# Two transformer layers on one core: the blocks' queries, keys and values in buffers of their own, and an earlier schedule for the attention sums

## The chip, the cores and the metric

One AWS Trainium2 chip, of which the kernel uses one core. A core has a matrix engine (TensorE; PE in the profile, its weight loads PEld), a vector engine (VectorE, DVE), a scalar engine (ScalarE, ACT), a general engine (GpSimd, POOL) and SyncE (SP), which here only issues transfers. Each engine works through its own list of instructions in order; semaphores tie the lists together. The metric is the device time of one launch in microseconds (us), as a median over runs. Tensors in use lie in on-chip memory of 128 partitions (SBUF), products of TensorE in a small accumulator memory (PSUM).

## The reference

The input `x` has 4 sequences of 1024 positions with 256 channels. Two layers follow each other, each added to its input:

```python
x = x + attention(layernorm(x))      # 16 heads of 16, causal, ALiBi bias, softmax over the positions
x = x + ffn(layernorm(x))

def ffn(x):                           # x: (4, 1024, 256); its attention runs along the FIRST axis
    q, k, v = split(x @ in_proj_w.T + in_proj_b)
    scores = einsum('tbhd,sbhd->bhts', q, k) / 4   # each of 1024 positions: 4 tokens among themselves
    ctx = softmax(scores) @ v
    h = layernorm(x + ctx @ out_w.T + out_b)
    probs = softmax(h @ router_w.T + router_b)     # 8 experts
    assign = max(index of the two largest)         # one expert for each token
    oe = gelu(h @ w1[assign].T + b1) @ w2[assign].T + b2
    return layernorm(h + oe)
```

The second layer therefore has two parts: an attention in which at each of the 1024 positions only its four tokens (one of each sequence) see each other, which is element-wise work of the vector engine, and a mixture of experts in which each of the 4096 tokens goes to exactly one of eight small networks (256 to 256 to 256).

## The kernel before

All of it is in `fast_layer`. (A general version, for inputs whose softmax sums leave a safe range, stands behind it in a branch that is not taken.)

**First layer.** Attention is cut into units: a chunk of 256 query positions of one sequence (16 of them); those of the last chunk are cut once more into blocks of 128, so there are 20 units. Each unit has four groups of four heads and, by the length of its keys, one or more rounds; there are 160 rounds in all. A round is `score` (TensorE makes scores `sk` from `slots`, ScalarE exponentiates them to `p`, GpSimd masks the diagonal at line 1005) and, two rounds at a time, `weigh` (TensorE multiplies `p` by the values `v`, ScalarE copies the result to `yt`). The values carry a column of ones, so the softmax's sums come out as rows of the same product. When a unit's last product is out, its result is normalised through DRAM in steps:

- `load_sums` (line 1064) stores `y` and loads the sums back in another layout, on SP's queue;
- `invert` (line 1071) takes reciprocals on VectorE and stores them (`r`, SP);
- `load_y` (line 1079) loads the reciprocals, spread over channels (`su`), and the unit's result (`yc`): four transfers on SP;
- `divide` (line 1096) multiplies `yc` by `su` on VectorE;
- `project` (line 1105) multiplies by the output weights on TensorE (`op`) and adds to `x` on VectorE.

SP's queue also carries the loads of keys and queries into `slots` (line 958) and the stores of keys. The very last unit is normalised on chip instead (`normalise`: a product `sum` with a constant, a reciprocal and a multiply for each group, `yn`; then `project_slots`).

**Second layer.** Positions are cut into 8 blocks of 128 positions with 4 tokens each. `front(i)` (line 1573) is a Python generator for one block; it yields between its stages and says which engine the next one needs: `E` and `P` for VectorE, `N` and `A` for ScalarE, `R` for GpSimd, `D` (and `d` for further pieces of the same) for TensorE. Its stages are in order: layer norm of `x` to `u`; transposes (`ut`); projection in four pieces, one for each token (`qkvp`, copied to `qkv`), where the first piece is of kind `DQ`; four score stages, one for each token t (a multiply `pr` and a reduce to `sc`); softmax over the four; four weighted products (`pv`, multiply and adds, to `ctx`); transposes (`ct`), output projection (`ao`), layer norm and the choice of the expert (`key`, `rank`, `hot`). In the last block (i = 7) some work stands differently: the values are projected between the score stages and ScalarE makes all copies, and TensorE sums the halves of the weighted products (`ctp`). A `DQ` piece may only be placed when no earlier block holds the flag `held["qkv"]`, since there is one `qkv` buffer of 4 x 776 floats in each partition. The block sets the flag at its `DQ` and takes it off after its fourth weighted product.

**Third part.** After 6 blocks have been placed, `tabulate_first` builds a table of 18 tiles of 128 tokens with equal expert; after the last block `tabulate_rest` builds the table of the other 20 (`counts_all`, `who`, `at_t`). Each of the 38 tiles is gathered (`given`, line 1839, an indirect transfer on GpSimd), transposed (`mtp`), multiplied (`hid`), put through gelu (`ge`), multiplied (`oe`), normalised (`o`) and scattered (`out_dram`, line 1955).

**What sets the order.** The order of instructions on every engine is fixed when the kernel is built, by a planner written in the kernel (main loop from line 2270). It goes through the 160 rounds in pairs and keeps estimated times of PE, DVE and ACT. Around the rounds it has places for vector work (`E_slot`, line 2219) and for TensorE work (`D_slot`, line 2231). At each place it issues what is due: the steps above of each unit, at set allowances after the unit's last product (the constants of line 76, in the planner's microseconds: sums 7, inverse 14, loads 18, multiply 29, projection 31), and then stages of at most two running blocks, vector ones by `take_E` (line 2076) and TensorE ones by `take_D` (line 2100). A block enters the queue when all four units over its positions are projected. So the allowances also set when blocks can begin.

After the last round the steps still due are issued, then groups 2 and 3 of the last unit are normalised (lines 2294 to 2301), and a second planner interleaves what is left: block 7, whatever of block 6 and of the first table is unfinished, and the tiles of the experts. There, the loads of the experts' weights stand on SP, for all experts in two layers (`w1`, `w2`) and for the first four tiles as sets of their own.

Of the kernel before, what the change touches and what calls it, by code (L numbers as in the profile page):

```python
# [37 lines left out]
P = 128  # L38
# [6 lines left out]
QC = 512  # L45
# [27 lines left out]
D_SLOT = 10.0  # L73
SWITCH, COLUMN, EXP_AT_ALL, EXP, READ = 0.2, 1 / 600, 0.17, 1 / 1200, 0.7
AHEAD, EARLY_BY, ROOT, OF_D = 1.0, 0.2, 1.4, 0.35
SUMS_BY, INVERTED_BY, Y_BY, DIVIDED_BY, PROJECTED_BY = 7.0, 14.0, 18.0, 29.0, 31.0

EXP_ZERO = -126 * math.log(2.0)

# [526 lines left out]
def fast_layer(ctx: ExitStack, tc: tile.TileContext, odd, x, wq, wk, wv, wp, w_in, w_out, w_r,  # L606
# [119 lines left out]
    def wide(a):  # L726
        return a.unsqueeze(1).to_broadcast([P, B] + list(a.shape)[1:])
# [4 lines left out]
    at_row = con(Q_ROW)  # L732
    number_i = const("number_i", [P, 1], I32)
    nc.gpsimd.iota(number_i, pattern=[[0, 1]], base=0, channel_multiplier=1)
    pos = fact.tile([P, T], F32, tag="pr", name="pos", bufs=2)
    nc.gpsimd.iota(
        pos, pattern=[[1, T]], base=-T // 2, channel_multiplier=0,
        allow_small_or_imprecise_dtypes=True,
# [728 lines left out]
    def prepare_biases(stage):  # L1467

        if stage == 0:
            b1_rows = fact.tile([E, C], F32, tag="equal", name="b1_rows")
            nc.scalar.dma_start(
                b1_rows.rearrange("e (c p) -> e c p", p=P),
                b1.rearrange("p (e c) -> e c p", c=CC),
            )
            b2_rows = fact.tile([E, C], F32, tag="before", name="b2_rows")
            nc.scalar.dma_start(b2_rows, b2)
            b_row = fact.tile([1, 2 * C], F32, tag="u", name="b_row", bufs=2)
            for k, at in enumerate((B_IN, B_OUT)):  # L1480
                nc.scalar.dma_start(
                    b_row[:, k * C:(k + 1) * C], rows[at:at + C].unsqueeze(0)
                )
            held["biases"] = (
                (b1_rows, b_bf[0]), (b2_rows, b_bf[1]),
                (b_row[:, :C], in_bf), (b_row[:, C:], out_bf),
            )
            return
        src, three = held["biases"][stage - 1]
        if three is out_bf:  # L1490
            nc.vector.tensor_tensor(src, src, router["passed"][0:1, :C], ALU.add)
        n, width = src.shape
        rest = fact.tile([n, width], F32, tag="pr", name="rest", bufs=2)
        nc.vector.tensor_copy(rest, src)
        pieces = fact.tile([n, 3, width], BF16, tag="turned", name="pieces", bufs=TURNED)
        for k in range(3):
            nc.vector.tensor_copy(pieces[:, k], rest)
            nc.sync.dma_start(three[k * n:(k + 1) * n, :width], pieces[:, k])
            if k < 2:
                nc.vector.tensor_tensor(rest, rest, pieces[:, k], ALU.subtract)  # L1500
# [72 lines left out]
    def front(i, fact, more, last):  # L1573
# [43 lines left out]
            for_later(t)  # L1617
        store(("x", i), store_later)
        yield "DQ" if more else "D", 2.8
        qkv = fact.tile([P, B, 3 * C + E], F32, tag="qkv", name=f"qkv_{i}")  # L1620

        def projected_qkv(t, lo, hi):
            pq = bank(f"qkvp_{i}_{t}")[:, :hi - lo]
            for cc in range(CC):
                nc.tensor.matmul(
                    pq, ut[:, cc, t * P:(t + 1) * P], w_in_sb[:, cc, lo:hi],
                    start=cc == 0, stop=cc == CC - 1,
                )
                if not lo + cc:
                    nc.tensor.matmul(pq[:, :C], ones_bf, in_bf, start=False, stop=False)  # L1630
            if lo and not last:
                nc.vector.tensor_copy(qkv[:, t, lo:hi], pq)
            else:
                nc.scalar.copy(qkv[:, t, lo:hi], pq)

        for t in range(B):
            projected_qkv(t, 0, QC)
# [4 lines left out]

        def routed():
            nc.vector.tensor_tensor(
                u_[:, :, C:], qkv[:, :, 3 * C:], wide(router["b_out"]), ALU.add
            )

        if not last:
# [4 lines left out]
        for t in range(B):  # L1653
            yield "E", 2.4, 0.9 if last else 0.0
            if last:
                projected_qkv(t, QC, 3 * C + E)
            pr = fact.tile([P, B, C], F32, tag="pr", name=f"pr_{i}_{t}", bufs=2)
            nc.vector.tensor_tensor(pr, wide(qkv[:, t, 0:C]), qkv[:, :, C:2 * C], ALU.mult)
            nc.vector.tensor_reduce(
                sc[:, t], pr.rearrange("p s (h d) -> p s h d", d=D), AX.X, ALU.add  # L1660
            )
        yield "E", 1.1
        over_s = lambda a: a.rearrange("p t s h -> p t h s")
        top = small.tile([P, B, H], F32, tag="top", name=f"top_{i}", bufs=1)
# [11 lines left out]
        nc.vector.tensor_tensor(sc, sc, each_s(tot), ALU.mult)  # L1676

        def weighted(t):
            pr = fact.tile([P, B, C], F32, tag="pr", name=f"pv_{i}_{t}", bufs=2)
            nc.vector.tensor_tensor(  # L1680
                pr.rearrange("p s (h d) -> p s h d", d=D),
                qkv[:, :, 2 * C:3 * C].rearrange("p s (h d) -> p s h d", d=D),
                sc[:, t].unsqueeze(3).to_broadcast([P, B, H, D]),
                ALU.mult,
            )
            return pr
# [26 lines left out]
        else:  # L1713
            ctx_ = fact.tile([P, B, C], F32, tag="ctx", name=f"ctx_{i}")
            for t in range(B):
# [1 line left out]
                pr = weighted(t)  # L1717
                nc.vector.tensor_tensor(pr[:, 0:2], pr[:, 0:2], pr[:, 2:4], ALU.add)
                nc.vector.tensor_tensor(ctx_[:, t], pr[:, 0], pr[:, 1], ALU.add)
        if more:  # L1720
            held.pop(("qkv",))
        if not last:
            if i < PC * (NC - 2):
                yield "N", 0
# [337 lines left out]
    def product(cost, what):  # L2062
        taken.clear()
        what()
        end = on_tensor(cost)
        busy("DVE", OF_D * cost, end - 0.5 * cost)
        read_at(max(end + READ, time["DVE"]))
        return end
# [28 lines left out]
                if it.kind == "end":  # L2097
                    running.remove(it)

    def take_D(cost):  # L2100

        for it in list(running):
            while it.kind[0] in "Dd":
                if it.kind == "DQ" and ("qkv",) in held:
                    break
                if it.kind != "d" and it.ready > time["PE"] + EARLY_BY:
                    break
                if cost and cost + it.cost > D_SLOT:
                    break
                if it.kind == "DQ":  # L2110
                    held["qkv",] = True
                cost += it.cost
                end = product(it.cost, it.next)
                it.ready = max(end + READ, time["DVE"])
            if it.kind == "end":
                running.remove(it)

    begins = [0]
# [109 lines left out]
            experts.fetch()  # L2228
        take_E(some)

    def D_slot(p):
        todo = of_D.pop(p, []) + pop_due(due_D, time["PE"])
        for cost, what in todo:
            product(cost, what)
        take_D(sum(cost for cost, _ in todo))

    for p in range(-6, 0):
        E_slot(2 * p)
# [34 lines left out]
    for p in range(len(rounds) // 2):  # L2273
        then = p < len(rounds) // 2 - 1
        score_next(2 * p)
        E_slot(2 * p)
        D_slot(p)
        fill()
        take_E(then)
        score_next(2 * p + 1)  # L2280
        if len(waiting) > 2:
            weigh_next(waiting[:2])
            del waiting[:2]
        fill()
        E_slot(2 * p + 1, then)
# [5 lines left out]


    assert not of_E and not of_D, (sorted(of_E), sorted(of_D))
    for _, what in pop_due(due_E + [], 1e9) + pop_due(due_D + [], 1e9):
        what()
    for it in running:
        it.ready = 0.0
    for g in range(2, G):
        normalise(g)
    load_sums(last_unit)  # L2300
    project_slots()
    tail = ctx.enter_context(pool("tail", 1))
# [205 lines left out]
```

## Time and profile before

| | |
|---|---|
| median of 3 runs (lowest to highest) | 827.63 us (824.45 to 828.9) |
| the profiled execution | 827.67 us |
| its span in the profile | 825.9 us |
| mean granted TensorE clock | 0.949 of full speed |
| busy: PE / weight loads / DVE / ACT / POOL | 708.6 / 532.4 / 544.8 / 416.5 / 253.6 us |
| last product of the attention's rounds ends | 620.4 us |
| block 7's first score multiply begins | 666.91 us |
| first gather of the second table | 734.32 us |

The span is the time from the first to the last instruction of the profiled execution; the device time of the same execution is 1.8 us longer. Busy times are averages over stages that differ a lot, so each stage has to be looked at by itself: 0 to 620 us is the first layer's attention with the blocks 0 to 6 of the second layer set in between; 620 to 734 is the rest of blocks 6 and 7 with the tiles of the first table; from 734 on there are only tiles. `L587` is the line of a helper through which nearly all instructions of the compute engines pass, so they are told apart by the names of their tiles. Names are written as out<-in.

### The profile page before, as it was taken

The page shows a single profiled execution, that of the slowest core. Times are in us where ns is not written, and L with a number is a line of the kernel's source. Part 1 is how long each engine was busy: PE and PEld are TensorE (multiplying, and loading weights), DVE is VectorE, ACT ScalarE, POOL GpSimd, SP SyncE. Part 2 cuts the span into 40 slices and gives each one's busy share as a digit, 9 for nine tenths or more (in the row PEclk, how much of TensorE's full clock was granted, in tenths as well). Part 3 has the DMA queues.
Part 4 walks back from the last instruction along what each step waited for, and adds up shares of the span by engine and source line. Part 5 has one row for each costly group of instructions (what it writes and reads, how often), then busy time and mean ns, then how long its engine had stood idle before and what let it go on. Part 6 is the DMA issues. An engine that isn't in the chain of part 4 may idle for free. (4 is left out here: it accounts for less than half of the span.)

```text
span 825.9 us, 22497 instructions
## 1 busy us (share of the span) xinstructions
PE 708.6 (86%) x8917; PEld 532.4 (64%) x8917; DVE 544.8 (66%) x1316; ACT 416.5 (50%) x625; POOL 253.6 (31%) x360
## 2 busy tenths in 40 slices
PE   3988878999999999998998998999983689677882
PEld 2766656667666656565787876788662368566771
DVE  7335403739489768847966648497684779885663
ACT  1554535647547656635665757487550236233540
POOL 5533211313021222111222211122120235638885
PEclk9899898999999999999999999999995699988996
DMA  7444444435234234423554556255125512234430
GB/s 218 120 149 147 115 126 139 137 98 169 82 105 136 91 97 127 131 74 98 140 157 118 163 162 158 57 156 166 36 75 198 178 47 89 89 96 127 128 97 25
DMA packets 75220, 99.57 MB, mean 121 GB/s; under 512 B 19496, under 2 KB 58723, under 8 KB 74596
## 3 DMA queue, kind: packets, MB, share of 16 engines
q1 hardware_dynamic: 62272, 67.84, 28.3%
q10 hardware_dynamic: 7972, 16.05, 6.2%
q0 software_dynamic: 4864, 14.16, 5.7%
q8 instruction: 73, 1.20, 0.7%
q14 instruction: 39, 0.32, 0.1%
HBM read 61.55 MB, written 35.12 MB: 117 GB/s over the span
## 5 line engine op out<-in xcount | busy, mean ns | idle before, releaser
L587 ACT ACTIVATE p<-sk 128x1024 f32<-128x1024 f32 (+1 forms) x320 | 287.8, 939 | 160.6 <-PE sk L587 139.4
L1005 POOL TENSOR_SCALAR_AFFINE_SELECT p<-p 128x512 f32<-128x512 f32 (+1 forms) x160 | 105.6, 664 | 396.6 <-ACT p L587 394.6
L587 PE MATMUL sk<-slots 32*128 32x128 f32 (+1 forms) x3456 | 181.1, 328 | 21.5 <-DVE kq L587 8.4
L587 PEld LDWEIGHTS sk<-slots 32*128 32x128 f32 x3456 | 137.2, 187 | 65.0 <-issue 24.8
L587 PE MATMUL pv<-p,v 128*32 128x128 f32 (+1 forms) x3456 | 143.4, 312 | 9.9 <-DVE count L587 2.9
L587 PEld LDWEIGHTS pv<-p,v 128*32 128x32 f32 x3456 | 95.9, 110 | 46.9 <-issue 7.8
L587 PE MATMUL qkvp<-w_in,ut 128*128 128x264 f32 (+1 forms) x228 | 80.3, 488 | 0.0
L587 PEld LDWEIGHTS qkvp<-w_in,ut 128*128 128x128 f32 x228 | 40.8, 193 | 26.9 <-issue 22.4
L587 PE MATMUL oe<-w,ge 128*128 (+1 forms) x152 | 43.4, 410 | 14.4 <-DVE given L587 6.0
L587 PE MATMUL qkp<-xt,wqk 128*128 128x256 f32 x224 | 55.5, 392 | 0.2 <-ACT p L587 0.2
L1839 POOL DMA_INDIRECT given<-rows,rows x38 | 43.5, 1144 | 27.4 <-DVE at_t L587 11.4
L587 DVE COPY qkv<-qkvp 128x264 f32<-128x264 f32 x28 | 12.1, 432 | 54.1 <-PE qkvp L587 54.1
L587 PEld LDWEIGHTS qkp<-xt,wqk 128*128 128x128 f32 x224 | 40.9, 191 | 10.5 <-issue 3.3
L587 PE MATMUL hid<-mt,w 128*128 128x128 f32 x304 | 47.2, 293 | 0.4 <-ACT ge L587 0.4
L587 ACT COPY qkv<-qkvp 128x512 f32<-128x512 f32 (+1 forms) x29 | 16.1, 557 | 59.0 <-PE qkvp L587 47.1
L587 PEld LDWEIGHTS hid<-mt,w 128*128 128x128 f32 x304 | 42.2, 201 | 1.9 <-ACT ge L587 0.9
L1955 POOL DMA_INDIRECT out_dram<-o,out_rows x38 | 38.9, 1024 | 8.7 <-issue 5.9
L587 DVE TENSOR_TENSOR pv<-qkv,sc 128x1024 f32<-128x1024 f32 x32 | 40.2, 1257 | 0.6 <-PE ctp L587 0.6
L587 DVE TENSOR_REDUCE sc<-pr 128x64 f32<-128x1024 f32 x32 | 39.0, 1220 | 1.1
L587 DVE TENSOR_TENSOR pr<-qkv 128x1024 f32<-128x1024 f32 x32 | 39.6, 1238 | 0.0
L587 PEld LDWEIGHTS oe<-w,ge 128*128 128x128 f32 x152 | 27.2, 200 | 19.1 <-DVE given L587 7.4
L587 PE MATMUL vp<-wv,xt 128*128 128x256 f32 x128 | 34.4, 414 | 0.0
(316 smaller groups left out, 1017.9 us busy)
## 6 DMA issues: line engine op xcount, KB each, us to landing
slots<-k SPq DMA_DIRECT2D x128, 80.0 KB
k<-kq SPq DMA_DIRECT2D x32, 256.0 KB
v<-v ACTq DMA_DIRECT2D x4, 1152.0 KB
x<-in_x_dram SPq DMA_DIRECT2D x16, 256.0 KB
y<-yt SPq DMA_DIRECT2D x16, 256.0 KB
rows<-x SPq DMA_DIRECT2D x32, 128.0 KB
slots<-k SPq DMA_DIRECT2D x64, 64.0 KB
rows<-u SPq DMA_DIRECT2D x8, 512.0 KB
```

The source lines that it names most:

```text
L587: ins = made(*args, **kwargs)
L1005: nc.gpsimd.affine_select(blocks, blocks, pattern=[[0, 2], [0, size], [1, P]], compare_op=ALU.is_ge, fill=0.0, base=0, channel_multiplier=-1,)
L1839: nc.gpsimd.indirect_dma_start(out=self.hx, out_offset=None, in_=t.rows_of, in_offset=bass.IndirectOffsetOnAxis(ap=t.rows_[:, self.j:self. ...
L1955: ins = nc.gpsimd.indirect_dma_start(out=out.rearrange("t n c -> (t n) c"), out_offset=bass.IndirectOffsetOnAxis(ap=t.table.out_rows[:, t. ...
```

## The change

It has five parts.

1. The five allowances of line 76 become 5, 10, 12.5, 19 and 20.5.
2. The buffer `qkv` is split into `qk` (queries and keys, one buffer, 4 x 512 floats a partition) and `vr` (values and the router's columns, two buffers of 4 x 264 floats). The flag `held["qkv"]` is taken off after the four score stages instead of after the four weighted products.
3. The scratch buffers tagged `pr` (also used once each by `pos` and `rest` in the preparation) go from two to one. In the last block, where TensorE reads the weighted products, every other one is put into the buffer tagged `ctx`.
4. `take_D` calls `take_E` after each TensorE piece of a block that it issues, so vector stages can be placed between pieces.
5. After the last round, the due vector steps are issued first, then `normalise` of groups 2 and 3, then the due projections; before, the projections stood ahead of `normalise`.

```diff
--- before.py
+++ after.py
@@ -73,7 +73,7 @@
 D_SLOT = 10.0
 SWITCH, COLUMN, EXP_AT_ALL, EXP, READ = 0.2, 1 / 600, 0.17, 1 / 1200, 0.7
 AHEAD, EARLY_BY, ROOT, OF_D = 1.0, 0.2, 1.4, 0.35
-SUMS_BY, INVERTED_BY, Y_BY, DIVIDED_BY, PROJECTED_BY = 7.0, 14.0, 18.0, 29.0, 31.0
+SUMS_BY, INVERTED_BY, Y_BY, DIVIDED_BY, PROJECTED_BY = 5.0, 10.0, 12.5, 19.0, 20.5
 
 EXP_ZERO = -126 * math.log(2.0)
 
@@ -732,7 +732,7 @@
     at_row = con(Q_ROW)
     number_i = const("number_i", [P, 1], I32)
     nc.gpsimd.iota(number_i, pattern=[[0, 1]], base=0, channel_multiplier=1)
-    pos = fact.tile([P, T], F32, tag="pr", name="pos", bufs=2)
+    pos = fact.tile([P, T], F32, tag="pr", name="pos")
     nc.gpsimd.iota(
         pos, pattern=[[1, T]], base=-T // 2, channel_multiplier=0,
         allow_small_or_imprecise_dtypes=True,
@@ -1490,7 +1490,7 @@
         if three is out_bf:
             nc.vector.tensor_tensor(src, src, router["passed"][0:1, :C], ALU.add)
         n, width = src.shape
-        rest = fact.tile([n, width], F32, tag="pr", name="rest", bufs=2)
+        rest = fact.tile([n, width], F32, tag="pr", name="rest")
         nc.vector.tensor_copy(rest, src)
         pieces = fact.tile([n, 3, width], BF16, tag="turned", name="pieces", bufs=TURNED)
         for k in range(3):
@@ -1617,7 +1617,8 @@
             for_later(t)
         store(("x", i), store_later)
         yield "DQ" if more else "D", 2.8
-        qkv = fact.tile([P, B, 3 * C + E], F32, tag="qkv", name=f"qkv_{i}")
+        qk = fact.tile([P, B, QC], F32, tag="qkv", name=f"qkv_{i}")
+        vr = fact.tile([P, B, C + E], F32, tag="vr", name=f"vr_{i}", bufs=2)
 
         def projected_qkv(t, lo, hi):
             pq = bank(f"qkvp_{i}_{t}")[:, :hi - lo]
@@ -1628,10 +1629,12 @@
                 )
                 if not lo + cc:
                     nc.tensor.matmul(pq[:, :C], ones_bf, in_bf, start=False, stop=False)
-            if lo and not last:
-                nc.vector.tensor_copy(qkv[:, t, lo:hi], pq)
+            if not lo:
+                nc.scalar.copy(qk[:, t], pq)
+            elif last:
+                nc.scalar.copy(vr[:, t], pq)
             else:
-                nc.scalar.copy(qkv[:, t, lo:hi], pq)
+                nc.vector.tensor_copy(vr[:, t], pq)
 
         for t in range(B):
             projected_qkv(t, 0, QC)
@@ -1642,7 +1645,7 @@
 
         def routed():
             nc.vector.tensor_tensor(
-                u_[:, :, C:], qkv[:, :, 3 * C:], wide(router["b_out"]), ALU.add
+                u_[:, :, C:], vr[:, :, C:], wide(router["b_out"]), ALU.add
             )
 
         if not last:
@@ -1654,11 +1657,14 @@
             yield "E", 2.4, 0.9 if last else 0.0
             if last:
                 projected_qkv(t, QC, 3 * C + E)
-            pr = fact.tile([P, B, C], F32, tag="pr", name=f"pr_{i}_{t}", bufs=2)
-            nc.vector.tensor_tensor(pr, wide(qkv[:, t, 0:C]), qkv[:, :, C:2 * C], ALU.mult)
+            pr = fact.tile([P, B, C], F32, tag="pr", name=f"pr_{i}_{t}")
+            nc.vector.tensor_tensor(pr, wide(qk[:, t, 0:C]), qk[:, :, C:], ALU.mult)
             nc.vector.tensor_reduce(
                 sc[:, t], pr.rearrange("p s (h d) -> p s h d", d=D), AX.X, ALU.add
             )
+
+        if more:
+            held.pop(("qkv",))
         yield "E", 1.1
         over_s = lambda a: a.rearrange("p t s h -> p t h s")
         top = small.tile([P, B, H], F32, tag="top", name=f"top_{i}", bufs=1)
@@ -1676,10 +1682,12 @@
         nc.vector.tensor_tensor(sc, sc, each_s(tot), ALU.mult)
 
         def weighted(t):
-            pr = fact.tile([P, B, C], F32, tag="pr", name=f"pv_{i}_{t}", bufs=2)
+            pr = fact.tile(
+                [P, B, C], F32, tag="ctx" if last and t % 2 else "pr", name=f"pv_{i}_{t}"
+            )
             nc.vector.tensor_tensor(
                 pr.rearrange("p s (h d) -> p s h d", d=D),
-                qkv[:, :, 2 * C:3 * C].rearrange("p s (h d) -> p s h d", d=D),
+                vr[:, :, 0:C].rearrange("p s (h d) -> p s h d", d=D),
                 sc[:, t].unsqueeze(3).to_broadcast([P, B, H, D]),
                 ALU.mult,
             )
@@ -1717,8 +1725,6 @@
                 pr = weighted(t)
                 nc.vector.tensor_tensor(pr[:, 0:2], pr[:, 0:2], pr[:, 2:4], ALU.add)
                 nc.vector.tensor_tensor(ctx_[:, t], pr[:, 0], pr[:, 1], ALU.add)
-        if more:
-            held.pop(("qkv",))
         if not last:
             if i < PC * (NC - 2):
                 yield "N", 0
@@ -2097,7 +2103,7 @@
                 if it.kind == "end":
                     running.remove(it)
 
-    def take_D(cost):
+    def take_D(cost, some):
 
         for it in list(running):
             while it.kind[0] in "Dd":
@@ -2111,8 +2117,10 @@
                     held["qkv",] = True
                 cost += it.cost
                 end = product(it.cost, it.next)
+
                 it.ready = max(end + READ, time["DVE"])
-            if it.kind == "end":
+                take_E(some)
+            if it.kind == "end" and it in running:
                 running.remove(it)
 
     begins = [0]
@@ -2228,11 +2236,11 @@
             experts.fetch()
         take_E(some)
 
-    def D_slot(p):
+    def D_slot(p, some=True):
         todo = of_D.pop(p, []) + pop_due(due_D, time["PE"])
         for cost, what in todo:
             product(cost, what)
-        take_D(sum(cost for cost, _ in todo))
+        take_D(sum(cost for cost, _ in todo), some)
 
     for p in range(-6, 0):
         E_slot(2 * p)
@@ -2274,7 +2282,7 @@
         then = p < len(rounds) // 2 - 1
         score_next(2 * p)
         E_slot(2 * p)
-        D_slot(p)
+        D_slot(p, then)
         fill()
         take_E(then)
         score_next(2 * p + 1)
@@ -2291,12 +2299,14 @@
 
 
     assert not of_E and not of_D, (sorted(of_E), sorted(of_D))
-    for _, what in pop_due(due_E + [], 1e9) + pop_due(due_D + [], 1e9):
+    for _, what in pop_due(due_E + [], 1e9):
+        what()
+    for g in range(2, G):
+        normalise(g)
+    for _, what in pop_due(due_D + [], 1e9):
         what()
     for it in running:
         it.ready = 0.0
-    for g in range(2, G):
-        normalise(g)
     load_sums(last_unit)
     project_slots()
     tail = ctx.enter_context(pool("tail", 1))
```

## The prediction

> **What bounds the kernel now.** I read the page's totals first, then the table of windows, then the waits, then the timelines of the engines at the end of attention. Windows give: stretch; its length; busy us (instructions) of PE, weight loads, DVE, ACT, POOL; the granted TensorE clock; DMA share; GB/s.
>
> ```profile
> PE 708.6 (86%) x8917; PEld 532.4 (64%) x8917; DVE 544.8 (66%) x1316; ACT 416.5 (50%) x625; POOL 253.6 (31%) x360
> 0.00:160.00 160.00, 127.67 (x1357) 94.88 (x1357) 75.33 (x217) 74.41 (x112) 53.83 (x93) 0.94 0.48 143
> 160.00:597.00 437.00, 417.75 (x6224) 303.60 (x6224) 306.89 (x666) 262.79 (x354) 87.10 (x125) 1.00 0.42 121
> 620.50:634.30 13.80, 6.33 (x16) 4.75 (x16) 4.82 (x12) 0.21 (x1) 0.00 (x0) 0.57 0.71 255
> 634.30:734.30 100.00, 75.69 (x471) 60.22 (x472) 84.36 (x231) 36.56 (x77) 37.83 (x38) 0.86 0.31 98
> 734.30:826.00 91.70, 61.49 (x413) 53.12 (x411) 53.47 (x161) 29.87 (x67) 69.13 (x99) 0.89 0.31 96
> ```
>
> The total for PE, 86%, hides four stages. From 160 to 597 us PE is busy 417.75 of 437 (96%): attention is bound by TensorE, and DVE, 306.89, has slack. From 620.5 to 634.3 every engine is below half: a chain of transfers after the last attention unit but one. From 634.3 to 734.3 DVE leads (84%): it finishes blocks 6 and 7 of the second layer. From 734.3 on POOL leads (69.13 of 91.7): gather and scatter of the expert tiles. So vector work taken out of the third stage shortens the run, and the same work put into attention costs little.
>
> Waits and timelines give the edges. The timeline rows are: start, duration, engine, line, operation, and in brackets the idle time before it and what ended it.
>
> ```profile
> DVE inverse L587 <- DMA sums<-y: 30.7, 6, 14.6
> DVE yc L587 <- DMA yc<-y: 19.2, 5, 6.7
> ...
> ACT qkv L587 <- DVE pv L587: 14.1, 2, 11.8
> ```
> ```profile
> 618.71 0.24 DVE L587 RECIPROCAL inverse<-sums 128x16 f32<-128x16 f32 x1
> 625.67 0.43 DVE L587 TENSOR_TENSOR yc<-yc,su 128x256 f32<-128x256 f32 x1 [6.71 <-DMA yc<-y]
> ...
> 632.57 0.42 DVE L587 TENSOR_TENSOR x<-x,op 128x256 f32<-128x256 f32 x1 [1.38 <-PE op L587]
> ...
> 666.91 1.22 DVE L587 TENSOR_TENSOR pr<-qkv 128x1024 f32<-128x1024 f32 x1
> ```
> ```profile
> 655.51 1.07 ACT L587 COPY qkv<-qkvp 128x512 f32<-128x512 f32 x2 [11.81 <-DVE pv L587]
> ```
> ```profile
> 734.32 1.00 POOL L1839 DMA_INDIRECT given<-rows,rows  x1 [11.43 <-DVE at_t L587]
> ```
>
> The reader is to see three things. DVE idles 50 us over the run for the returning `sums` and `yc`. Block 7's queries and keys sit in PSUM until block 6's last weighted product (`pv`, 654.21) has released the only `qkv` buffer: 11.81 us. The last stage starts when the table of tiles is ready (734.32).
>
> **The change, part by part.** Both kernels issue nearly the same instructions (about 1,255 vector and 2,850 TensorE ones by their order), so its price is in the order.
>
> *Buffers.* Block 7's DQ piece may now start after block 6's four scores, not after its four weighted products, and `vr` has two buffers. What blocked ACT for 11.81 us is gone. Cost nothing by itself: the same copies stand on the same engines. Single `pr` scratch: multiply, reduce and weighted adds are all DVE and in order, so no wait arises; only block 7's weighted product is read by PE (`ctp`), and there it alternates with the `ctx` buffer, two buffers as before. If that cover failed, each of four products would wait for two transposes, about 1 us: 4 us at most.
>
> *Vector stages between pieces, and shorter times.* In the order of the changed kernel the second layer's blocks run earlier inside attention: unit 3's addition to `x`, which lets the first blocks begin, comes at round 29 of 160, not 33. By the end of attention block 5 and the table of the first 18 tiles are done, and block 6 has two of four weighted products. Before, that stood behind attention. In the order listing the vector work that leaves the stages after 618 us is, at the timeline's durations:
> - `own`, `full_of`, `late`: 1.25; `top` and subtraction: 0.95
> - `before_of` to `whose`: 1.98; `tot` to `sc`: 1.54; `in_tile`: 1.4
> - two weighted products with their sums: 2 x 2.32 = 4.64
> - `who_f` to `at_w`: 2.65
>
> Sum 14.4 us. In attention, DVE has 130 us free between 160 and 597, so its price there is only what it delays. `who_first` moves 1.3 us of PE into attention; a 2.86 us PE wait for `count` before the last product goes. I put attention's end at 618.3, against 620.4.
>
> *The chain at the end, walked in the new order.* `inverse` of unit 18, at 618.71, stood behind 3 us of table work and a late round: now about 614. From there to the multiply is 6.96 us in the trace, about 6.7 with fewer neighbours in the queue: 620.7. The last addition to `x` follows 7 us later (two `op`, `sum`, `yn`, as before): 627.7. Then come `pv` of t=2 (2.3), the table's preparation (0.9) and four statistics (2.3): `rstd_u` 633.2, before 637.38. Transposes and copies of `u` took 6 us from there: 640. Then block 7's queries and keys: four pieces with nothing to wait for, each 1.02 + 0.27 on PE, behind `ao` of block 6 and the first expert products (`mtp`, `hid`, about 3 us): all copied at 649, before 665. The first score was at 666.91 with 1.8 us of `u`, `ao` between; now 653.4, since `pv` of t=3, `ct` and block 6's statistics are put ahead. From here the four scores with the router's small operations between take 17 us as before: subtraction of the maximum 670.3 (684.2). The softmax and four weighted products of block 7 with no block 6 work between them, 686 (709.4 to the last); `u` plus `ao` 688.3 (711.7). Then DVE has 3 us more than before (expert outputs and `stats_v` were placed after `ao`), so the key, rank and table chain, 12.1 us from `u` to `hot`, ends at 703.4 (723.8). From `hot` to the first gather of the last table is 10.5 us in the trace and the same instructions: 713.9 against 734.32, 20.4 us earlier. From that gather on POOL's order, PE's from the counts on, and DVE's from `hot` are identical: 91.6 us again.
>
> Span: 713.9 + 91.6 = 805.5. The profiled execution is 827.67 for a span of 825.9, 1.8 around it: 807.3. It stands on the median of 827.63, so no correction: 807.
>
> *Where rules of the skill are weighed.* The row from the inverse to the multiply is 6.96 us, and it holds two transfers in turn, the inverse's store and the reloads. The Trainium skill, "DMA: Bandwidth & Descriptors", section "Anatomy of one DMA — SWDGE (gpsimd) path", gives about 2 us fixed for one DMA, so an estimate of two is 4 us; the trace adds the four issues (0.57 to 0.60 each on SP, 621.19 to 623.72). By the rule a vector engine that comes to the multiply after 4 us would find its data; by the row it waits 2.5 to 3 us more. That speaks against the shorter times: they put the multiply two to three rounds after the inverse, not three to six. A round is about 3.9 us (620 / 160), so at two rounds the cover is 7.8 us, just above the row. I take the row: 3 us for such waits over attention, all reaching PE. Bounds: 0 (they only eat DVE slack), and 16 units x 0.65 = 10.
>
> *Its other risk.* Vector stages between product pieces put 1 to 2.5 us of block work ahead of `kq` copies and `yn`. I take +3 (0 to 10). Against these, the hole of the first chunk boundary. DVE was held there by the `sums` of unit 3, behind the slot loads on SP:
>
> ```profile
> 125.40 0.35 DVE L587 RECIPROCAL inverse<-sums 128x32 f32<-128x32 f32 x1 [14.57 <-DMA sums<-y]
> ```
> ```profile
> 127.28 2.19 PE L587 MATMUL sk<-slots 32*128 32x256 f32 x16 [8.26 <-DVE passed L587]
> ```
>
> In the new order unit 3's sums load stands one filling of slots further ahead, so of the 8.26 us (and of 5.85 in a hole before it) some may vanish: 0 to 8, I take 5. Plus 3, plus 3, minus 5 makes 1 us, within the reading error of the walk: 807 stays.
>
> **The rivals.**
> - *Half of the tail's gain is eaten.* Expert products and the loads of own weights (0.5 MB a tile) now stand earlier on PE and SP, next to block 7's copies; the clock is low there (0.57 at 620 to 634). For it: PE was busy 75.7 of 100 us in that stage and would have the same in 80. Against it: PE needs block 7 only every 2.7 us a tile. A gain of 10: 817.
> - *Attention shortens too.* The boundary hole goes wholly (8.26) and half of the wait at 5.85 with it, no delays arise: 807 - 1 - 8 = 798. For it: PE is busy only 127.67 of the first 160. Against it: SP's queue still carries slot loads there.
> - *Nothing moves the end.* The blocks are done sooner, yet `x` of the last unit is as late as before and block 7's vector chain as long. Against: 14.4 us of vector work provably stands ahead of attention's end in the new order. It would give 826.
> - *Slower, by the sums.* With the allowance for the sums at 5 rather than 7, `inverse` comes to the vector engine while `sums` are still behind the slot loads on SP, as in the 14.57 us row, and everything behind it (`kq` copies of the next chunk) waits. The place is the chunk boundaries, units 7, 11 and 15, which had 0 to 1.0 us of such wait. Each new hole costs PE 8.26. Three: 807 + 24.8 = 832, slower; it decides from three holes on, or 1.5 us a unit over 16 units. For it: the DMA waits of 50 us already there. Against: DVE's slack of 130 us, and that the loads themselves are issued earlier too.
>
> **How the numbers follow.** Likeliest, 0.53: 807, own range 800 to 815. Attention shorter too, 0.12: 798. Half eaten, 0.17: 817, of which 0.03 reaches 824 to 828. Nothing moves, 0.04: 826. Slower by holes, 0.14: 832 to 840, of which 0.02 ends at 828 to 832. What this kernel's measurement can tell is about 0.5%, 4.1 us: faster below 823.5, slower above 831.8. Faster 0.53 + 0.12 + 0.14 = 0.79; same 0.03 + 0.04 + 0.02 = 0.09; slower 0.12. For 8 in 10 the range leaves out the slower case above and the low end of the shorter attention: 796 to 828.
>
> **What would show it.** Right: ACT's 11.81 us wait for `pv` is gone; `who_first` runs before attention ends; the first gather of the last table lies about 20 us sooner and about 92 us before the span's end; the stage between attention's end and that gather is near 96 us, before 114. Wrong: attention's end later than 625, with DVE waits for `sums` or `yc` above 50 us and PE gaps for `kq`; or block 7's first score not before 660.

## The result, and the profile after

The changed kernel takes 838.26 us (median of 4 runs, 835.5 to 840.85) against 827.15 for the kernel before on the same chip: a ratio of 1.0137, 95% interval 1.0088 to 1.0186. It is slower by about 11 us; the forecast was 807, with a range that ended at 828.

The page's total and the table of windows of the changed kernel, cut at the end of the last product of attention's rounds (656.8) and at the first gather of the second table (746.0). Columns as before: stretch; length; busy us (instructions) of PE, weight loads, DVE, ACT, POOL; granted clock; DMA share; GB/s.

```profile
PE 720.3 (86%) x8917; PEld 540.4 (64%) x8917; DVE 546.5 (65%) x1316; ACT 416.6 (50%) x625; POOL 250.7 (30%) x360
0.00:656.80 656.80, 583.11 (x8043) 426.79 (x8043) 417.58 (x951) 350.76 (x482) 144.06 (x224) 0.95 0.41 118
656.80:746.00 89.20, 73.41 (x467) 58.95 (x464) 75.59 (x205) 36.22 (x77) 37.17 (x39) 0.96 0.44 147
746.00:838.50 92.50, 63.80 (x413) 54.63 (x411) 53.36 (x161) 29.64 (x67) 69.49 (x99) 0.88 0.31 96
```

The kernel before, cut at the same events:

```profile
0.00:620.40 620.40, 565.06 (x8019) 414.32 (x8019) 402.19 (x914) 349.81 (x481) 146.59 (x223) 0.98 0.43 125
620.40:734.30 113.90, 82.02 (x487) 64.97 (x488) 89.18 (x242) 36.83 (x78) 37.83 (x38) 0.83 0.36 117
```

The totals of the two pages differ by little and don't tell where the time went; the stages do. The second stage became 24.7 us shorter (113.9 to 89.2) and the third stayed (91.7 to 92.5). Attention became 36.4 us longer. In it TensorE idled 18.4 us more (55.3 to 73.7, length less busy) and was also 18.1 us longer busy, at a lower granted clock (0.98 to 0.95), with 24 matmuls more (`who_first`, 0.82 us, which stood behind attention before). So the loss lies wholly in attention.

The waits of the changed kernel (engine, line, what it waited for: us in total, times, longest):

```profile
DVE yc L587 <- DMA yc<-y: 52.5, 11, 9.6
...
DVE inverse L587 <- DMA sums<-y: 8.9, 2, 5.8
```

VectorE's wait for the sums fell from 30.7 us to 8.9, and its wait at the multiply rose from 19.2 to 52.5 (57.5 with 5.0 at one multiply that the view puts down to another transfer; the table below has all of it). Of the 19.2, 6.7 came after attention's end, of the 57.5, 4.7. The wait behind it on TensorE, idling that ended with a multiply of `yc`, is smaller: 20.6 us over the run, against 7.5 before. The worst one shows how it comes about. VectorE's timeline, then SyncE's queue, then TensorE, all of the changed kernel (start, duration, operation, idle time before it and what ended it):

```profile
89.44 0.41 DVE L587 TENSOR_SCALAR slots<-slots,low_con,q_by 128x256 f32<-128x256 f32 x1
99.41 0.69 DVE L587 TENSOR_TENSOR yc<-yc,su 128x512 f32<-128x512 f32 x1 [9.56 <-DMA yc<-y]
```
```profile
88.35 2.10 SPq L1498 DMA_DIRECT2D b_bf<-pieces  x3
90.54 0.39 SPq L1075 DMA_DIRECT2D r<-inverse  x1
91.02 1.82 SPq L1498 DMA_DIRECT2D in_bf<-pieces  x3
92.94 0.65 SPq L1090 DMA_DIRECT2D su<-r  x1
93.64 0.64 SPq L1093 DMA_DIRECT2D yc<-y  x1
...
94.94 0.57 SPq L1093 DMA_DIRECT2D yc<-y  x1
```
```profile
91.01 1.99 PE L587 MATMUL vp<-wv,xt 128*128 128x256 f32 x8
100.16 3.78 PE L587 MATMUL vp<-wp,yc 128*128 128x256 f32 x8 [7.15 <-DVE yc L587]
```

The inverse was made at 82.7; its store left SP only at 90.54, behind other transfers; the last reload was issued at 94.94 and had landed by 99.41, 16.7 us after the inverse. VectorE had 6.0 us of other work to do in between and then stood. The unit's projection stands in TensorE's list right behind a value product, so TensorE stood too, 7.15 us. (The bank that the projection writes into is named `vp` in this row; the operands `wp,yc` tell what it is.) And when it came, its eight matmuls took 3.78 us, while the eight before the wait took 1.99.

### The profile page after: what moved, and what is told of

It reads as the page before. It is cut to its first block, busy times and chain, and to the rows that moved or that the text cites. A ratio compares the mean times of both kernels' runs of the same rounds, so it can differ in the third digit from the quotient of the medians.

```text
span 838.5 us, 22488 instructions
## 1 busy us (share of the span) xinstructions
PE 720.3 (86%) x8917; PEld 540.4 (64%) x8917; DVE 546.5 (65%) x1316; ACT 416.6 (50%) x625; POOL 250.7 (30%) x360
## 5 line engine op out<-in xcount | busy, mean ns | idle before, releaser
L1005 POOL TENSOR_SCALAR_AFFINE_SELECT p<-p 128x512 f32<-128x512 f32 (+1 forms) x160 | 101.5, 637 | 472.4 <-ACT p L587 470.8
L587 PE MATMUL sk<-slots 32*128 32x128 f32 (+1 forms) x3456 | 184.8, 333 | 20.5 <-ACT p L587 9.4
L587 PEld LDWEIGHTS sk<-slots 32*128 32x128 f32 x3456 | 139.8, 192 | 66.1 <-issue 28.8
L587 PE MATMUL pv<-p,v 128*32 128x128 f32 (+1 forms) x3456 | 148.0, 320 | 6.4 <-ACT p L587 2.3
L587 PEld LDWEIGHTS pv<-p,v 128*32 128x32 f32 x3456 | 98.7, 113 | 45.0 <-issue 10.6
L587 PE MATMUL qkvp<-w_in,ut 128*128 128x264 f32 (+1 forms) x220 | 73.8, 474 | 0.0
L587 DVE TENSOR_TENSOR yc<-yc,su 128x512 f32<-128x512 f32 (+1 forms) x19 | 12.1, 635 | 57.5 <-DMA yc<-y 52.5
L587 PE MATMUL op<-wp,yc 128*128 128x256 f32 x84 | 25.3, 445 | 18.7 <-DVE yc L587 8.3
L587 DVE TENSOR_TENSOR pv<-vr,sc 128x1024 f32<-128x1024 f32 x32 | 39.6, 1237 | 0.3
L587 PEld LDWEIGHTS oe<-w,ge 128*128 128x128 f32 x152 | 27.1, 199 | 17.3 <-DVE mv_v L587 7.5
L587 DVE COPY vr<-qkvp 128x264 f32<-128x264 f32 x28 | 12.1, 432 | 38.2 <-PE qkvp L587 38.1
```

What stands on the lines that cost most here:

```text
L587: ins = made(*args, **kwargs)
L1005: nc.gpsimd.affine_select(blocks, blocks, pattern=[[0, 2], [0, size], [1, P]], compare_op=ALU.is_ge, fill=0.0, base=0, channel_multiplier=-1,)
```

## The experiments

The theories were: **T**, VectorE comes to the multiply before `yc` and `su` have landed, because of the shorter allowances; **V**, the vector stages between product pieces delay what TensorE waits for; **Q**, the earlier release of the queries' buffer crowds TensorE; and, from the second group on, **O**, the new order itself is the loss and the waits are only its symptom.

All runs in one table, each ratio against the kernel before on the same chip (medians there 827.09 to 828.18): end of attention, length of the second and third stage, the idle time before all 19 multiplies in VectorE's timeline (each from one profiled execution, us), then median and ratio to the kernel before with its interval. In the rows "multiply at 24" and "at 29" the projection is moved along (25.5, 31).

| kernel | attention | second | third | idle at the multiply | median | ratio |
|---|---|---|---|---|---|---|
| before | 620.4 | 113.9 | 91.7 | 19.2 | 827.15 | |
| changed | 656.8 | 89.2 | 92.5 | 57.5 | 838.26 | 1.0137 (1.0088 to 1.0186) |
| before + short allowances | 658.8 | 110.2 | 92.2 | 60.5 | 863.31 | 1.0453 (1.0371 to 1.0534) |
| changed, old allowances | 626.2 | 112.0 | 91.4 | 26.1 | 830.35 | 1.0020 (1.0002 to 1.0039) |
| changed, no stages between | 664.8 | 104.0 | 91.9 | 61.7 | 865.59 | 1.0452 (1.0382 to 1.0522) |
| changed, buffers and end only | 628.8 | 112.9 | 91.6 | 17.3 | 833.35 | 1.0064 (1.0044 to 1.0084) |
| changed, multiply without wait | 617.8 | 89.1 | 92.3 | 0 | 799.51 | 0.9635 (0.9605 to 0.9664) |
| changed, yc loaded early | 639.8 | 90.2 | 92.6 | 35.6 | 824.42 | 0.9957 (0.9935 to 0.9979) |
| changed, multiply at 24 | 632.8 | 101.4 | 91.7 | 23.8 | 826.38 | see below |
| changed, multiply at 29 | 621.3 | 104.4 | 91.1 | 2.2 | 816.01 | 0.9831 (0.9775 to 0.9886) |
| before, only sums, inverse and loads early | 616.6 | 109.3 | 92.6 | 0 | 817.78 | 0.9877 (0.9841 to 0.9914) |
| changed, at 29, no stages between | 614.8 | 111.7 | 91.7 | 4.4 | 821.84 | 0.9945 (0.9919 to 0.9970) |
| changed, at 29, yc early | 619.1 | 104.3 | 91.1 | 0.8 | 816.49 | 0.9875 (0.9836 to 0.9913) |
| changed, at 24, yc early | 627.6 | 104.5 | 92.2 | 14.4 | 818.64 | 0.9888 (0.9847 to 0.9929) |

### Which part of the change costs the time

The short allowances alone:

```diff
-SUMS_BY, INVERTED_BY, Y_BY, DIVIDED_BY, PROJECTED_BY = 7.0, 14.0, 18.0, 29.0, 31.0
+SUMS_BY, INVERTED_BY, Y_BY, DIVIDED_BY, PROJECTED_BY = 5.0, 10.0, 12.5, 19.0, 20.5
```

> The kernel before with the five shorter allowances alone. Theory T (times): the vector engine comes to the multiply before yc has landed and stands there (yc waits 52.5 us in the changed kernel, 19.2 before), TensorE then waits and attention grows; attention ends at 645 to 660, yc waits above 40 us, total 845 to 860 since the shorter tail is missing. Theory V (vector stages between pieces delay kq and yn): no change here, 827 within 5. Theory Q (the earlier start of a block's projections crowds TensorE in attention): 827 within 5.

It took 863.31 us, attention ended at 658.8. The waits and windows of this kernel:

```profile
DVE yc L587 <- DMA yc<-y: 58.9, 12, 11.3
```
```profile
0.00:658.80 658.80, 582.43 (x8019) 425.30 (x8019) 402.79 (x923) 349.27 (x481) 152.00 (x223) 0.94 0.41 118
658.80:769.00 110.20, 81.17 (x487) 64.91 (x488) 88.32 (x234) 36.75 (x78) 38.88 (x38) 0.83 0.36 119
```

This is all of the changed kernel's loss in attention, without its gain behind it. Its attention window has just as many TensorE instructions as that of the kernel before (8019), yet is busy 582.43 us against 565.06: 17 us of the loss are the same matmuls at a lower clock. The short allowances are enough for the loss; neither V nor Q is needed for it.

The changed kernel with the old allowances:

```diff
-SUMS_BY, INVERTED_BY, Y_BY, DIVIDED_BY, PROJECTED_BY = 5.0, 10.0, 12.5, 19.0, 20.5
+SUMS_BY, INVERTED_BY, Y_BY, DIVIDED_BY, PROJECTED_BY = 7.0, 14.0, 18.0, 29.0, 31.0
```

> The changed kernel with the allowances of before (7, 14, 18, 29, 31). T: attention ends again near 620 to 628, yc waits near 20 us, the tail stays 20 or more shorter: 800 to 812. V and Q: attention still ends near 655: 833 to 840.

Attention is back at 626.2, as T said. But the second stage is back too, 112.0, so the total is 830.35, not 800 to 812. T was right on the loss and wrong on where the gain comes from: at the old allowances the split buffers and the stages between pieces shorten the second stage by only 2 us. ScalarE's 11.8 us wait for `pv` does not appear in this kernel's waits, and still block 7's first score begins at 669.4, against 666.9 before. Counted from attention's end it comes 3.3 us sooner (43.2 for 46.5), so little came of the 11.8 us.

The changed kernel without stages between pieces:

```diff
                 it.ready = max(end + READ, time["DVE"])
-                take_E(some)
```

> The changed kernel without vector stages between pieces (allowances short, buffers split). T: 830 to 842, yc waits still above 40 us. V: attention ends near 620 to 630, 805 to 815. Q: 833 to 840.

865.59 us, waits of 61.7. V is the wrong way round: the stages between pieces save 27 us here (22 in the profiled executions: 8.0 of attention and 14.8 of the second stage, less 0.6 of the third). T had expected at most 842 and did not see that.

Neither short allowances nor stages between (both edits above on the changed kernel):

> The changed kernel with neither the short allowances nor the stages between pieces: the split buffers, the earlier release and the order at the end remain. T and V: attention ends near 620, the 11.8 us wait of ScalarE for pv is gone: 810 to 820. Q: attention ends near 650 and the total is 830 or more.

833.35, attention 628.8: Q is out as the cause of the large loss. So are the 810 to 820 that I expected from the buffers alone. This kernel is even a little slower than the one before (1.0044 to 1.0084), by 8.4 us of attention; which of its parts costs that was not tried.

### Taking the wait away in the same order

Here the order of instructions on every engine is that of the changed kernel (name by name in the two traces), but the multiply's operands are always there. It leaves out the division by the softmax's sums, and its reloads of `yc` go unread at a quarter of the width.

```diff
     def load_y(u):
...
-            nc.sync.dma_start(yc[:, cc], heads_of(u)[at, :D])
+            nc.sync.dma_start(part_yc[:, cc], heads_of(u)[at, :D, :64])
...
     def divide(u):
-        yc, su = held["y", u]
-        nc.vector.tensor_tensor(yc, yc, su, ALU.mult)
+        width = units[u][2] * P
+        yc = ends.tile([P, CC, W], F32, tag="yc", name=f"yc_{u}", bufs=2)[:, :, :width]
+        nc.vector.tensor_tensor(yc, wp_sb[:, :, :width], wp_sb[:, :, :width], ALU.mult)
```

> The changed kernel, in the same order of instructions on every engine, but the multiply no longer waits for transfers: it multiplies two halves of the output weights into yc. It leaves out the division by the softmax sums (the inverse, its store and the su loads stay; the yc loads stay as four-times narrower ones into a buffer that nobody reads). T (the vector engine standing at yc is the whole loss): attention ends at 618 to 630 instead of 656.8, the granted clock in attention is back at 0.97 or more, total 798 to 812. O (the new order itself crowds TensorE, waits are only a symptom): attention still ends after 645, total 826 or more.

799.51 us. The windows of this kernel:

```profile
0.00:617.80 617.80, 569.20 (x8043) 417.64 (x8043) 416.36 (x952) 349.86 (x482) 143.28 (x224) 0.97 0.42 121
617.80:706.90 89.10, 73.67 (x463) 58.83 (x464) 75.20 (x204) 36.13 (x77) 37.11 (x39) 0.96 0.44 147
706.90:799.20 92.30, 63.96 (x413) 54.59 (x411) 53.59 (x161) 29.52 (x67) 69.50 (x99) 0.88 0.31 96
```

Attention is 39.0 us shorter than in the changed kernel, the two later stages are the same to 0.2 us. O is out. Of the 39.0, 25.1 is less idling of TensorE (73.7 to 48.6) and 13.9 less busy time of the same 8043 instructions. (What the narrower reloads give by themselves was not separated. The kernels below whose reloads are whole and whose multiply comes late end attention at 614.8 to 621.3 too, but in another order.) The place shown above reads, in this kernel:

```profile
91.59 1.99 PE L587 MATMUL vp<-wv,xt 128*128 128x256 f32 x8
93.42 1.89 PE L587 MATMUL vp<-wp,yc 128*128 128x256 f32 x8
```

The projection of unit 1 begins at 93.42 without a wait and takes 1.89 us, not 3.78.

### Where the multiply may stand

> The changed kernel with the multiply and projection at 29 and 31 as before; sums, inverse and loads stay early. T: yc waits under 15 us, attention ends at 615 to 628; blocks begin as late as before, tail 108 to 114: 820 to 832. If the early sums or the early loads on SP are the loss: attention ends after 645 all the same.

```diff
-SUMS_BY, INVERTED_BY, Y_BY, DIVIDED_BY, PROJECTED_BY = 5.0, 10.0, 12.5, 19.0, 20.5
+SUMS_BY, INVERTED_BY, Y_BY, DIVIDED_BY, PROJECTED_BY = 5.0, 10.0, 12.5, 29.0, 31.0
```

816.01, faster than both kernels, and better than T's 820 to 832. The early sums and loads are no loss; the early multiply, with its projection, is. Windows of this kernel:

```profile
0.00:621.30 621.30, 572.11 (x8043) 420.02 (x8043) 407.87 (x940) 350.02 (x481) 144.31 (x224) 0.97 0.43 125
621.30:725.70 104.40, 78.92 (x464) 64.60 (x464) 82.84 (x216) 36.80 (x78) 36.52 (x38) 0.84 0.37 125
```

The same five numbers in the kernel before (multiply and projection stay where they were, only sums, inverse and loads come sooner):

> The kernel before with only the first three allowances shortened (5, 10, 12.5; multiply and projection stay at 29 and 31). T: the multiply finds its data (waits under 5 us), attention ends at 615 to 622, tail as before (110 to 114): 818 to 826. If early sums and loads hurt by themselves: above 832.

817.78, just below T's 818 to 826. Here the waits at the multiply are gone altogether (19.2 to 0), and with them 3.8 us of attention and 4.6 of the second stage. The one line that sets the allowances, set so, gives nearly everything that any version gained that computes the whole layer. Its windows:

```profile
0.00:616.60 616.60, 567.48 (x8019) 415.91 (x8019) 401.04 (x915) 350.07 (x481) 147.52 (x223) 0.97 0.44 126
616.60:725.80 109.20, 82.55 (x485) 64.04 (x485) 88.78 (x241) 36.51 (x77) 38.26 (x38) 0.84 0.37 120
```

Without the stages between pieces, multiply at 29:

> The changed kernel with multiply and projection at 29 and 31 and without vector stages between pieces. Stages between pieces fill attention's vector engine and take work out of the tail: without them 820 to 830, tail 108 or more against 104.4. If they are worth nothing where nothing waits: 816 within 4.

821.84, second stage 111.7: the stages between pieces are worth 6 us here by the medians. The two profiled executions differ by 1.4 us only (7.3 us less second stage and 0.6 less third for 6.5 us longer attention); the one of this kernel was 2 us faster than its median, the other 2.5 us slower. The expectation is met.

The `yc` loads behind the sums load, in the changed kernel, at its own allowances, at 24 and 25.5, and at 29 and 31:

```diff
     def load_sums(u):
...
+        yc = ends.tile([P, CC, W], F32, tag="yc", name=f"yc_{u}", bufs=2)[:, :, :width]
+        for cc in range(CC):
+            nc.sync.dma_start(yc[:, cc], heads_of(u)[some * cc:some * (cc + 1), :D])
     def load_y(u):
...
-            nc.sync.dma_start(yc[:, cc], heads_of(u)[at, :D])
```

> The changed kernel with the two yc loads issued right behind the sums load, so that only the two su loads follow the inverse's store. T: two issues of 0.6 us leave the chain from inverse to multiply, so each of 11 waits shrinks by about 1.2 us, up to 13 us in all: 822 to 834. If the length of that chain does not matter: 838 within 4.

824.42: the idle time at the multiply fell from 57.5 to 35.6, 21.9 us where I had expected up to 13, and attention by 17.0. Two issues fewer behind the inverse make 1.2 us for each of 11 waits; what the rest of the shrinkage comes from I did not separate. The total is within its expectation.

> The changed kernel with the yc loads behind the sums load and with multiply and projection at 29 and 31. T: the multiply had 2.2 us of waits left, so the earlier loads bring little: 813 to 819. If SP's queue behind the loads matters, more than 5 us either way.

816.49: nothing left to gain where the multiply does not wait (816.01 without it).

> The changed kernel with the yc loads behind the sums load and with multiply and projection at 24 and 25.5. T: waits of 5 to 20 us, attention ends at 620 to 630, tail 98 to 103: 808 to 822; best if the waits stay under 8 us.

818.64: waits of 14.4 us and attention to 627.6, as expected; the second stage of 104.5 is not (98 to 103). The profiled execution was the slowest of the four, 7 us above the median. In between is no better than late.

The multiply at 24 with the `yc` loads where they were:

> The changed kernel with the multiply and projection at 24 and 25.5, half way back; sums, inverse and loads stay early. T: yc waits fall from 57 to 20 to 40 us, attention ends at 630 to 645, blocks start later again so that the tail is 95 to 110: 820 to 838. O: as the changed kernel, 835 to 842.

Two of its twelve runs took 812 and 819 us, the other ten 825 to 831, so no ratio is given; the cause of the spread is open. The profiled execution, one of the ten, has 23.8 us of waits at the multiply, attention to 632.8 and a second stage of 101.4: between its neighbours at 19 and 29, as T says.

## Why the prediction was wrong

**The second and third stage: right, with the gain undersized.** The work named in the list did leave: VectorE's busy time in the second stage fell from 89.18 to 75.59, 13.6 us, for 14.4 forecast. The table's product runs inside attention now (first line), and the first gather of the second table is 89.2 us after attention's end, not the 95.6 of the walk (second line):

```profile
631.28 0.82 PE L587 MATMUL who_first<-in_tile,at_place 128*128 128x54 bf16 x24
```
```profile
745.97 1.01 POOL L1845 DMA_INDIRECT given<-rows,rows  x1 [10.00 <-DVE at_t L587]
```

The walk was too long up to block 7's first score: that comes 29.2 us after attention's end, for 35.1 in the walk. The third stage is 92.5 for 91.6. Had attention ended at the 618.3 of the forecast, these two stages would have given a span of 800 us; the kernel whose multiply does not wait ends attention at 617.8 and has a span of 799.2.

**The step that failed: "I take the row: 3 us for such waits over attention, all reaching PE", with its upper bound of 10.** Against the kernel whose multiply does not wait it measured 39.0 us. The 3 us was not worked out: a cover of 7.8 us against a row of 6.96 gives no wait at all. Three errors stand behind it.

- *One mean stood for all units.* As a mean the cover was right: in the kernel whose multiply does not wait, it comes 7.7 us after the inverse (mean of 19). But single units have from 1.4 to 12.4 us, and a unit with time to spare gives none to the next. Eight of them have less than 6.96 us; an estimate from these distances, each held against 6.96, is 25 us of waits of VectorE. With the multiply at 29 the time from inverse to multiply, less the wait itself, is 18 to 19 us in the mean, in the kernel before 13.4.
- *The chain was read in a quiet place.* 6.96 us is from the end of attention. The 12 multiplies that waited in the changed kernel came 6.1 to 16.7 us after the inverse, 10.7 in the mean. In the longest, the store and the reloads stood behind other transfers on SP, as the rows at 90 us show.
- *A wait of TensorE was priced at its length only.* The same product of 128x256 takes longer after a wait. The view of the tile `yc` in the changed kernel (duration min/median/max in ns) has the projections of most units first, and then the one that came after 7.15 us of idling; below it are windows of the changed kernel from that projection on (the granted clock is third from the end), and one of the same projection in the kernel without the wait:

```profile
L587 PE MATMUL op<-wp,yc x84: 379/379/767, 85.8 to 659.4; 128*128 128x256 f32 x84
...
L587 PE MATMUL vp<-wp,yc x8: 634/634/794, 100.2 to 103.3; 128*128 128x256 f32 x8
```
```profile
100.10:104.00 3.90, 3.84 (x12) 2.66 (x12) 0.03 (x2) 0.00 (x0) 0.00 (x0) 0.50 0.27 78
104.00:108.00 4.00, 4.00 (x64) 2.75 (x64) 2.20 (x7) 2.17 (x4) 1.12 (x2) 0.76 0.60 164
```
```profile
93.40:95.40 2.00, 2.00 (x13) 1.49 (x15) 0.05 (x1) 0.96 (x2) 0.00 (x0) 1.00 0.10 16
```

At a granted clock of 0.50 the product took 634 ns, at 1.00 it took 379. Over attention the lower clock comes to 13.9 of the 39.0 us: by the clock records of the two traces TensorE was at half clock for 71.7 us of attention in the changed kernel and for 34.1 us in the one without the wait. The Trainium skill, "TensorE: Matmul & The Clock Gate", Part 1, has TensorE at half clock after a window of about 3.4 us of idling, and back at full clock after about as long a busy one. The trace agrees that a wait is followed by half clock; here it lasted until 5.8 us after work had resumed (0.50 up to 104, then 0.76 over 4 us). I had used a granted clock of 0.57 to describe the end of attention and did not put such a term into the price of new waits.

"All reaching PE" was wrong the other way: VectorE waited 57.5 us, and TensorE idled 25.1 us more.

**The rule that was weighed.** By the rule the data would have been there after 4 us, by the row after 6.96; the runs say 10.7 where the multiply waits. The measurements decide, against the rule and against my row. The section quoted is on transfers that GpSimd issues, and these were issued by SyncE, so the 4 us was a weak guide from the start.

**"Its other risk", plus 3 for the stages between pieces: the wrong sign at these allowances.** Without them attention is 8.0 us longer. With the multiply at 29 they do lengthen it, by 6.5, and give 7.3 back in the second stage.

**"Against these, the hole of the first chunk boundary": the gain is there, but the fall of the sums' waits is not it.** The wait of 14.57 us for the sums of unit 3 and TensorE's hole of 8.26 us are gone, and the sums' waits fell from 30.7 to 8.9 us. But in the same order without the wait at the multiply they are 21.7 us, so more than half of the fall goes with the wait at the multiply, which makes VectorE late for the next inverse. There the hole stands one unit earlier and is shorter (VectorE, then TensorE):

```profile
107.70 0.35 DVE L587 RECIPROCAL inverse<-sums 128x32 f32<-128x32 f32 x1 [10.38 <-DMA sums<-y]
```
```profile
108.70 1.77 PE L587 MATMUL sk<-slots 32*128 32x256 f32 x12 [5.13 <-issue]
```

In the kernel before with early sums and loads (817.78) VectorE waits 34.0 us for the sums. That wait was no measure of the loss.

**The rivals.** The slower one gave 832 to 840, and 838 is what came, but by another mechanism. It put the loss at the sums behind the slot loads at three chunk boundaries, and the sums' waits shrank. "Against: DVE's slack of 130 us" was no argument: the slack was real, but VectorE works through its list in order, and a wait in it also holds what TensorE needs next. The rivals of a half eaten tail gain and of an unmoved end are refuted by the second stage. That attention would also shorten beyond the 618.3 of the forecast does not hold even without the wait: 617.8.

**The signs.** Those of being wrong came, with `yc`: attention's end at 656.8, 52.5 us of waits, block 7's first score at 686.0. Of those of being right, the gather 20 us sooner did not (it is 11.7 us later).

**ScalarE's 11.81 us wait.** It is gone as forecast. The run with the old allowances shows that its going was worth little by itself, and "cost nothing by itself" is not shown for the buffers: with the new order at the end and nothing else they made a ratio of 1.0064. The gain of the second stage takes the short allowances and the stages between together: without the first it is 112.0 us long, without the second 104.0, with both 89.2. What the buffers add to the two was not tried apart.

**The count of instructions.** The 1,255 and 2,850 are not those of the traces, which have 1316 vector and 8917 TensorE instructions in both kernels; that the two are alike holds.

## What to carry to other kernels

An instruction that waits for a transfer is to be placed by the time that its own engine takes to come to it, read from that engine's timeline for each instance, and held against the transfer's longest time, not a quiet one. A mean over instances hides the short ones. In this kernel it paid to start the steps of the chain early (the sums, the inverse, the loads) and to leave the consumer late: that alone, on one line of the kernel before, gave 817.78 for 827.09. And a new wait on the way of TensorE is to be priced with its length and the slower matmuls behind it, here about 14 us on top of 25. The 799.51 us without the wait shows what is left to look for: the short second stage needs the early multiply, and no kernel here that computes the whole layer had both that and no wait.

## What the runs showed of the hardware that I had not expected

The clock's part was larger than I would have guessed: between the kernel before and the same with the short allowances, both with 8019 TensorE instructions there, attention had 17.4 us more busy time when 21.0 us of idle time was spread through it (76.3 us against 55.3).
